# Moving loads, stores, reciprocals, rotations and late products between the steps of an attention and FFN layer

## The chip, the cores and the metric

The kernel runs on 1 core of one Trainium2 chip. The metric is the device time of one execution, in microseconds (us). The engines are called as the profile calls them: PE (TensorE, matmuls), PEld (its weight loads), DVE (VectorE), ACT (ScalarE), POOL (GpSimd), SP (SyncE, which here issues every DMA). "SPq" is SP's queue.

## What is computed

One pre-norm transformer layer over 8 sequences of 512 tokens with 512 features: attention with low-rank projections of queries, keys and values (16 heads, 128 features without and 64 with rotary position), then a gated FFN with weights rounded to 8 bits. Cut to what matters:

```python
def attn(h, wq_a, q_norm_w, wq_b, wkv_a, kv_norm_w, wkv_b, wo):   # h: 8 x 512 x 512
    q = rmsnorm(h @ wq_a.T, q_norm_w)                             # 384
    q_nope, q_pe = split((q @ wq_b.T).reshape(b, s, 16, 192), 128)
    kv_c, k_pe = split(h @ wkv_a.T, 128)
    k_pe = rope(k_pe)                                             # one for all heads
    k_nope, v = split((rmsnorm(kv_c, kv_norm_w) @ wkv_b.T).reshape(b, s, 16, 256), 128)
    q_pe = rope(q_pe)
    scores = einsum("bqhd,bkhd->bhqk", cat(q_nope, q_pe), cat(k_nope, k_pe)) / sqrt(192)
    out = einsum("bhqk,bkhd->bqhd", softmax(scores), v)
    return out.reshape(b, s, 2048) @ wo.T

def ffn(x, ...):                                                  # wq: weights rounded to e4m3
    return ((silu((x @ gate_wq) * gate_s) * ((x @ up_wq) * up_s)) @ down_wq) * down_s

x = x + attn(layernorm(x), ...)
x = x + ffn(layernorm(x), ...)
```

## The kernel before

The kernel does the attention of all 8 batches first (`attention`) and then the FFN of all 8 (`ffn`). The weights of queries and keys, and of values and output, are multiplied together in batch 0 (`fold_q`, `fold_o`), so that scores and products run on the latents themselves. The layer's input and the attention's result pass through DRAM.

**Steps.** Attention is one loop over 512 steps, `steps = (batch, head, tile of 128 queries)`: 64 steps a batch, 4 a head. Step numbers below count from the start of a batch. In each step the function `scores` puts three matmuls of 512 columns on PE (L529 and, for the rotary part in two halves, twice L531), a maximum over keys on DVE (`nmax`, L533) and the exponential with its sum on ACT (L536). The `rest` of a step, the reciprocal of the sum (L540), the scaling (L541) and a transpose in 32 x 32 blocks (L163), is recorded at the beginning of the next step. After every second tile, so at the start of even steps, `send` writes the block of transposed probabilities to DRAM (`way<-block`, L173) and reads it back in its final place in four DMAs (`prT<-way`, L175).

**All else is hung onto steps.** `put(i, f)` adds a piece of work to step i, to be recorded after that step's scores, in the order of the `put` calls; `at(b, h, t)` gives a step's number. The loop runs inside `manual_schedule`: the order in which instructions are recorded is the order of every engine's queue, and of SP's. The pieces that the change touches:

- `attend(b, h)` multiplies a head's probabilities with the values (`av`, L552), 5 steps after its last tile, and needs both halves of `prT`.
- `project` (qn, L517) and `project_pe` (qpe, L489) make the next queries. `project_pe` runs 6 steps before an even head, for two heads, and calls `rope` at once: a shuffle and two products on DVE (L394 to L396), a sum on POOL (L397). `hi` (ACT, L500) and `lo` (DVE, L505) then split the result in two parts, one step later each.
- `output(b, g)` makes, per group of 4 heads, seven products (Strassen's scheme: u, z, u, v, u, v, u; 4 matmuls of 256 columns each, L597), each followed on DVE by a sum into the batch's x (L601). A product u needs the sum of the u before it, as both use one PSUM buffer. They stand 7, 8, 12 and 15 steps after the group's last tile. For group 0 the first ones are in steps 22 and 23. `store` writes x to DRAM after the last group, at 13 and 16.
- `latents(b)` makes the next batch's latents during this batch: `moments` (L141), `deviation` (Sqrt on ACT, reciprocal on DVE, step 18), centring, transposing and projecting tile by tile (heads 7, 8, 11, 12), `norms` (Sqrt on ACT and reciprocal on DVE, L448 to L451, step 52), `scale` (L454, L457, steps 53 and 54), `transpose_l` (`lat_pt` on PE, L464, steps 54 and 55), `rotary` for the keys (step 56).
- `round_piece` rounds one half of an FFN weight tile in batches 1 to 6, every 4 steps: load, `first` (DVE and POOL), the rest (L81 and L82, DVE), and a store (L381). Its input and output tiles alternate in two buffers, so L82 of a piece must wait for the store of the piece before.
- `load_wst` fetches a group's output weights (1.8 MB in four DMAs, two buffers); `load_x` fetches a batch's x in four tiles, once as `x` (residual) and once as `tok` (for the latents of the next batch, or, in the last batch, for the first FFN).
- `load_ffn` fetches rounded weights: `wg` in the last batch, the first half of `wu` (1.5 MB) in its last step.

PSUM has eight buffers: six in a ring (`ps_r`) for everything in attention but the products, one for u, one for v and z. In `ffn`, each of 12 slices has a gate and an up product (8 matmuls each, L817) in PSUM pools of their own, then the down products (L843).

Of the kernel before, what the change touches and what calls it, by code (L numbers as in the profile page):

```python
# [43 lines left out]
P = 128  # L44
# [42 lines left out]
class Layer:  # L87
    def __init__(self, ctx, tc, ins, out):
        self.tc, self.nc, self.ins, self.out = tc, tc.nc, ins, out
        nc = self.nc  # L90
        self.wp = ctx.enter_context(tc.tile_pool(name="w", bufs=1))
        self.xp = ctx.enter_context(tc.tile_pool(name="x", bufs=1))
# [38 lines left out]
    def ln_stats(self, x, small):  # L131
# [16 lines left out]
        return moments, deviation, mv, rstd  # L148

# [30 lines left out]
    def ffn_stats(self, x, small):  # L180

        moments, deviation, mv, rstd = self.ln_stats(x, small)
        for t in range(NT):
            moments(t)
        deviation()

# [13 lines left out]
    def ffn_normed(self, x, small, psum, work):  # L200
# [3 lines left out]
        yh, yl = self.ffn_parts()  # L204
        moments, deviation, mv, rstd = self.ln_stats(x, small)
        got = {}
# [12 lines left out]

        return moments, deviation, apply, transpose, (yh, yl)  # L220

    def ffn_normed_blocks(self, x, y, small, work):
# [27 lines left out]
        return stats, apply, send, split, (yh, yl)  # L250

    def attention(self):
        tc, nc, ins, wp, xp = self.tc, self.nc, self.ins, self.wp, self.xp
        with ExitStack() as ctx:
            fp = ctx.enter_context(tc.tile_pool(name="a_f", bufs=2))
            hp = ctx.enter_context(tc.tile_pool(name="a_h", bufs=2))
            sp = ctx.enter_context(tc.tile_pool(name="a_s", bufs=4))

            ps_r = ctx.enter_context(tc.tile_pool(name="ps_r", bufs=6, space=PSUM))
            ps_o = ctx.enter_context(tc.tile_pool(name="ps_o", bufs=1, space=PSUM))  # L260
# [141 lines left out]
            def latents(b):  # L402
# [11 lines left out]
                got = {}  # L414
                moments, deviation, mv, rstd = self.ln_stats(x, sp)

# [51 lines left out]
                def rotary():  # L468
# [8 lines left out]
                    f.__name__: f  # L477
                    for f in (moments, deviation, center, transpose_x, project_x, norms, scale, transpose_l, rotary)
                }
                return pieces, (lat, kvt, kpe)  # L480

            def project_pe(b, pair):
# [14 lines left out]
                def hi():  # L497
                    qpe = state["pe", b, pair] = hp.tile([P, 2, S], F32R, tag="qpe", name="qpe")
                    for k in range(2):
                        nc.scalar.copy(qpe[half[k], k, :], rotated[half[k]])  # L500

                def lo():
                    qpe = state["pe", b, pair]
                    for k in range(2):
                        nc.vector.tensor_tensor(  # L505
                            qpe[half[1 - k], k, :], rotated[half[k]], qpe[half[k], k, :], ALU.subtract
                        )

                return hi, lo

# [134 lines left out]
            for t in range(1, NT):  # L645
                p0["moments"](t)
            p0["deviation"]()
            for t in range(NT):
# [3 lines left out]
                p0["project_x"](t)  # L652
            p0["norms"](), p0["scale"](0)
            for t in range(NT):
# [65 lines left out]

            def put_stats(b, moments, deviation):
                for t, i in enumerate((at(b, 3), at(b, 3, 1), at(b, 3, 3), at(b, 4, 1))):
                    put(i, moments, t)
                put(at(b, 4, 2), deviation)

            def put_latents(b):
                p, state["latents", b] = latents(b)
                put_stats(b - 1, p["moments"], p["deviation"])
                for t, h in enumerate(tile_heads):
                    put(at(b - 1, h), p["center"], t)  # L730
                    put(at(b - 1, h, 1), p["transpose_x"], t)
                    put(at(b - 1, h, 3), p["project_x"], t)
                put(at(b - 1, 13), p["norms"])
                for t in range(NT):
                    put(at(b - 1, 13, 1) + t // 2, p["scale"], t)
                    put(at(b - 1, 13, 2) + t // 2, p["transpose_l"], t)
                put(at(b - 1, 14), p["rotary"])

            def put_ffn():
                moments, deviation, apply, transpose, self.y = self.ffn_normed(self.fx[0], sp, ps_r, hp)  # L740
                put_stats(B - 1, moments, deviation)
                for t, h in enumerate(tile_heads):
# [4 lines left out]
            for b in range(1, B + 1):  # L747
                to, key, src = (toks, b, hidden(b)) if b < B else (self.fx, 0, self.x2[0])
                for k, f in enumerate(load_x(to, key, src, wp, "tok")):
                    put(at(b - 1, 2, 1) + 2 * k, f)  # L750
                put(at(b - 1, 3), *((put_latents, b) if b < B else (put_ffn,)))
            for g in range(NG):
                put(at(B - 1, G * g + 3, 1), self.load_ffn, "wg", g, wp, f"wa{g}")
            put(at(B - 1, NH - 1, 3), self.load_ffn, "wu", 0, wp, "wst", 2)

            with tc.manual_schedule():
                prT = block = rest = None
                for i in range(len(steps) + 17):
                    if rest:
# [21 lines left out]
    def ffn(self):  # L781
        tc, nc, ins, xp = self.tc, self.nc, self.ins, self.xp
        with ExitStack() as ctx:
            wp = ctx.enter_context(tc.tile_pool(name="f_w", bufs=1))
            qp = ctx.enter_context(tc.tile_pool(name="f_q", bufs=2))
            ps_g = ctx.enter_context(tc.tile_pool(name="ps_g", bufs=2, space=PSUM))
            ps_u = ctx.enter_context(tc.tile_pool(name="ps_u", bufs=2, space=PSUM))
            ps_d = ctx.enter_context(tc.tile_pool(name="ps_d", bufs=2, space=PSUM))

            gs, us, ds = self.gs, self.us, self.load_w("ds", pool=wp)  # L790
# [9 lines left out]
            for b in range(B):  # L800
# [10 lines left out]
                for i in range(NI):  # L811
                    pg = ps_g.tile([P, S], F32, tag="g", name="pg")
                    pu = ps_u.tile([P, S], F32, tag="u", name="pu")
                    for ps, name in ((pg, "wg"), (pu, "wu")):
                        for c in range(NC):
                            for k in range(2):
                                nc.tensor.matmul(  # L817
                                    ps,
                                    w[name, i][:, c * P : (c + 1) * P],
                                    y[k][:, c, :],  # L820
                                    start=c == 0 and k == 0,
                                    stop=c == NC - 1 and k == 1,
                                )
                    gate = qp.tile([P, S], F32, tag="gate", name="gate")
# [14 lines left out]
                for t in range(NT):  # L839
                    pd = ps_d.tile([P, H], F32, tag="d", name="pd")  # L840
                    for i in range(NI):
# [76 lines left out]
```

## Time and profile before

| | us |
|---|---|
| three timed runs | 2830.87, 2823.72, 2834.58 (median 2830.87) |
| the profiled execution | 2823.94, of it 2822.2 in the span of the profile |
| attention (until the last product on values) | about 2283 |
| FFN | about 540 |
| one batch of attention | about 280 |
| DVE busy in the span | 1862.8 |
| ACT busy in the span | 902.9 |

A line of the profile's groups or of its timeline has the engine, the line of the kernel, the operation, and its result and sources; "x8" is a number of instructions, and each fp32 matmul counts as two. What stands in brackets at the end is the idle time before it on its engine, and what ended that wait. Three groups show how the attention's inner work looks (busy us, mean ns of one, idle us before them and its releaser):

```profile
L531 PE MATMUL sc<-kpe,qpe 128*128 128x512 f32 x1024 | 526.4, 595 | 2.1 <-DVE qpe L505 2.1
L552 PE MATMUL av<-prT,kvt 128*128 128x512 f32 x1024 | 469.3, 601 | 27.4 <-DMA prT<-way 24.6
L163 DVE STREAM_TRANSPOSE block<-pr 128x512 f32<-128x512 f32 x512 | 364.3, 711 | 17.7
```

### The profile page before, as it was taken

To read this page: it belongs to the slowest core of one execution; us is meant where nothing else is said; L and a number is where in the kernel's file an instruction comes from. 1 tells how busy PE (TensorE), PEld (TensorE's weight loads), DVE (VectorE), ACT (ScalarE), POOL (GpSimd) and SP (SyncE) were. 2 spreads that over 40 slices of the span, in tenths; PEclk is the share of its full clock that TensorE was granted. 3 is DMA by queue.
4 is the path that set the end of the run, shared out by engine and by line. 5 is a ranking of instruction groups with operands and counts; after the bars stand their busy time and mean duration, and the time that the engine had idled before them with its cause. 6 is when DMAs were issued, how large, how long until landed. Compare 5 with 4: busy or idle time off the path is not lost.

```text
span 2822.2 us, 29110 instructions
## 1 busy us (share of the span) xinstructions
PE 2739.9 (97%) x9264; PEld 1724.0 (61%) x9264; DVE 1862.8 (66%) x3680; ACT 902.9 (32%) x1956; POOL 575.5 (20%) x629
## 2 busy tenths in 40 slices
PE   8999999999999999999999999999999979999999
PEld 4555555555555555655555555555555568888887
DVE  5766777777777777777777777777767724343332
ACT  3333333333333333333333333333332323332222
POOL 1222222112221222122212221222111112222222
PEclk9999999999999999999999999999999989999999
DMA  3655465546544654465446545554565542111110
GB/s 113 208 185 166 159 199 174 161 145 200 180 147 157 196 176 146 157 197 175 146 160 197 173 144 170 188 173 146 163 199 181 175 170 81 60 60 64 64 64 19
DMA packets 262376, 426.07 MB, mean 151 GB/s; under 512 B 29648, under 2 KB 192592, under 8 KB 260688
## 3 DMA queue, kind: packets, MB, share of 16 engines
q1 hardware_dynamic: 262224, 424.21, 46.5%
q8 instruction: 74, 1.21, 0.2%
q14 instruction: 78, 0.64, 0.1%
HBM read 248.99 MB, written 175.11 MB: 150 GB/s over the span
## 4 chain that ended last, share of the span: by engine, by line
PE 84%; DVE 8%; DMA 4%; ACT 1%; SPq 1%; issue 1%; POOL 0%; ACTq 0%; DVEq 0%; POOLq 0%
PE av L552 14%; PE sc L529 12%; PE qn_ps L517 9%; PE u_ps L597 7%; PE sc L531 7%; PE pg L817 6%; PE pd L843 6%; PE pu L817 6%; PE qpe_ps L489 5%; PE lr_ps L431 4%; PE v_ps L597 4%; DMA way<-block 2%; PE z_ps L597 2%; DVE pr L541 1%; DVE block L163 1%; DVE nmax L533 1%
## 5 line engine op out<-in xcount | busy, mean ns | idle before, releaser
L536 ACT ACTIVATE pr<-sc,nmax 128x512 f32<-128x512 f32 x512 | 352.0, 687 | 1270.2 <-DVE nmax L533 1270.1
L531 PE MATMUL sc<-kpe,qpe 128*128 128x512 f32 x1024 | 526.4, 595 | 2.1 <-DVE qpe L505 2.1
L529 PE MATMUL sc<-lat,qn 128*128 128x512 f32 x1024 | 524.2, 593 | 1.1 <-ACT qn L519 1.1
L552 PE MATMUL av<-prT,kvt 128*128 128x512 f32 x1024 | 469.3, 601 | 27.4 <-DMA prT<-way 24.6
L533 DVE TENSOR_REDUCE nmax<-sc 128x1 f32<-128x512 f32 x512 | 337.9, 660 | 74.0 <-PE sc L531 72.8
L163 DVE STREAM_TRANSPOSE block<-pr 128x512 f32<-128x512 f32 x512 | 364.3, 711 | 17.7
L541 DVE TENSOR_SCALAR pr<-pr,rden 128x512 f32<-128x512 f32 x512 | 343.1, 670 | 18.1
L517 PE MATMUL qn_ps<-lat,wa 128*128 128x512 f32 x768 | 350.3, 592 | 0.0
L531 PEld LDWEIGHTS sc<-kpe,qpe 128*128 128x128 f32 x1024 | 194.7, 190 | 248.0 <-issue 238.1
L552 PEld LDWEIGHTS av<-prT,kvt 128*128 128x128 f32 x1024 | 195.9, 192 | 231.7 <-issue 221.4
L529 PEld LDWEIGHTS sc<-lat,qn 128*128 128x128 f32 x1024 | 189.5, 190 | 141.1 <-issue 120.3
L397 POOL TENSOR_TENSOR roped<-rope_own,rope_sw 128x512 f32<-128x512 f32 x72 | 91.7, 1274 | 697.5 <-DVE rden L540 620.2
L517 PEld LDWEIGHTS qn_ps<-lat,wa 128*128 128x128 f32 x768 | 145.3, 189 | 134.5 <-issue 123.0
L831 POOL TENSOR_TENSOR fl<-fuse,fh 128x512 fp32r<-128x512 f32 x96 | 126.2, 1314 | 386.2 <-ACT fh L830 386.2
L827 DVE SCALAR_TENSOR_TENSOR fuse<-pu,us,gate 128x512 f32<-128x512 f32 x96 | 71.9, 749 | 197.8 <-PE pu L817 193.1
L489 PE MATMUL qpe_ps<-lat,wqp 128*128 128x512 f32 x384 | 175.1, 592 | 0.0
L76 POOL TENSOR_TENSOR q_r<-raw,q_m 128x256 f32<-128x256 f32 x72 | 53.3, 740 | 594.8 <-DVE q_m L74 530.7
L540 DVE RECIPROCAL rden<-den 128x1 f32<-128x1 f32 x512 | 80.3, 157 | 121.5 <-ACT pr L536 118.0
L817 PE MATMUL pg<-yh,wg 128*128 128x512 f32 x384 | 149.6, 390 | 0.0
L817 PE MATMUL pg<-yl,wg 128*128 128x512 f32 x384 | 149.4, 389 | 0.0
L817 PE MATMUL pu<-yh,wu 128*128 128x512 f32 x384 | 149.4, 389 | 0.0
L817 PE MATMUL pu<-yl,wu 128*128 128x512 f32 x384 | 149.4, 389 | 0.0
(115 smaller groups left out, 3674.1 us busy)
## 6 DMA issues: line engine op xcount, KB each, us to landing
way<-block SPq DMA_DIRECT2D x256, 512.0 KB, 2.6
prT<-way SPq DMA_DIRECT2D x1024, 128.0 KB, 2.8
wst<-wst_d SPq DMA_DIRECT2D x56, 512.0 KB, 4.5
wst<-wst_d SPq DMA_DIRECT2D x56, 384.0 KB, 3.7
x<-in_hid SPq DMA_DIRECT2D x60, 256.0 KB, 4.1
x<-x SPq DMA_DIRECT2D x16, 512.0 KB, 4.6
out<-o SPq DMA_DIRECT2D x32, 256.0 KB, 2.0
wst_d<-wst SPq DMA_DIRECT2D x8, 896.0 KB, 4.6
```

The source lines that it names most:

```text
L163: self.nc.vector.transpose(out[:, :, :, i : i + Q].rearrange("p c k i -> p k c i"), x.rearrange("p (k c j) -> p k c j", c=NQ, j=Q),)
L489: nc.tensor.matmul(ps, wqp_s[g][:, r, pj * P : (pj + 1) * P], lat[:, r, :], start=r == 0, stop=r == NR - 1)
L517: nc.tensor.matmul(ps, wa_s[g][:, j, r, :], lat[:, r, :], start=r == 0, stop=r == NR - 1)
L529: nc.tensor.matmul(sc, qn[:, q], lat[:, NR, :], start=True, stop=False)
L531: nc.tensor.matmul(sc, qpe[:, h % 2, q], kpe[:, part, :], start=False, stop=part == 1)
L533: nc.vector.tensor_reduce(nmax, sc, AX.X, ALU.max, negate=True)
L536: nc.scalar.activation(pr, sc, AF.Exp, bias=nmax, accum_out=den)
L541: nc.vector.tensor_scalar(pr, pr, rden, None, ALU.mult)
L552: nc.tensor.matmul(av, kvt[:, kt, :], prT[:, :, :, kt, :], start=kt == 0, stop=kt == NT - 1)
L597: nc.tensor.matmul(got[name][:, t, :], ops[p][left][:, t * P : (t + 1) * P], w[:, p, right, :], start=first and t == 0 and p == 0, stop=la ...
L817: nc.tensor.matmul(ps, w[name, i][:, c * P : (c + 1) * P], y[k][:, c, :], start=c == 0 and k == 0, stop=c == NC - 1 and k == 1,)
L843: nc.tensor.matmul(pd, f[:, i, t * P : (t + 1) * P], w["wd", i], start=i == 0 and f is fh, stop=i == NI - 1 and f is fl,)
```

## The change

It moves work between steps; PE, DVE, ACT and the DMAs do the same operations on the same data.

- Loads of `wst` come 8 steps later, `tok` 8 steps earlier (steps 1, 3, 5, 7), the four tiles of `x` in steps 17, 18, 20, 21 instead of 16 to 19.
- The stores of rounded weights come one step earlier, x's last store one step later.
- `deviation` and `norms` lose their reciprocals to `deviation_inverse` and `norms_inverse`, one step later. The four `scale` stay; `transpose_l` and `rotary` come one step later.
- `project_pe` returns `rotate, hi, lo`, so that each comes one step later.
- In the last batch, three of the seven products of group 2 go to steps 65 and 66, behind the last scores. The first part of `wu` is loaded in step 66, and in step 67, ahead of the last `attend` (step 68), the gate products of FFN slices 0 and 1 are computed with the new function `hidden`. `ffn` uses them when it comes to these slices.
- The six-buffer PSUM ring now belongs to the layer and also serves the FFN, in place of three pools of two.

```diff
+    def hidden(self, name, i, y):
+        ps = self.ps_r.tile([P, S], F32, tag="r", name="pg" if name == "wg" else "pu")
+        for c in range(NC):
+            for k in range(2):
+                self.nc.tensor.matmul(
+                    ps,
+                    self.ffn_w[name, i][:, c * P : (c + 1) * P],
+                    y[k][:, c, :],
+                    start=c == 0 and k == 0,
+                    stop=c == NC - 1 and k == 1,
+                )
+        return ps
...
         def deviation():
             nc.scalar.activation(sd, mv[:, :, 1], AF.Sqrt, bias=self.eps_ln)
+
+        def deviation_inverse():
             nc.vector.reciprocal(rstd, sd)
...
+                def norms_inverse():
                     nc.vector.reciprocal(rms, rms)
...
-                rotated = rope(ps, 1.0)
+                rotated = []
+
+                def rotate():
+                    rotated.append(rope(ps, 1.0))
...
                     def rotary_part():
-                        hi, lo = project_pe(b, h // 2)
-                        put(i - 5, hi)
-                        put(i - 4, lo)
+                        for k, f in enumerate(project_pe(b, h // 2)):
+                            put(i - 5 + k, f)
...
-                        for n, f in zip((7, 8, 12, 13, 15, 16), output(b, g)):
+                        when = (7, 8, 18, 13, 19, 17) if (b, g) == (B - 1, NG - 2) else (7, 8, 12, 13, 15, 17)
+                        for n, f in zip(when, output(b, g)):
                             put(i + n, f)
...
-                        put(at(b, G * g + 3, 3) - 14 + 2 * k, f)
+                        put(at(b, G * g + 3, 3) - 6 + 2 * k, f)
                 for k, f in enumerate(load_x(xs, b, hidden(b), xp, "x")):
-                    put(at(b, 4) + k, f)
+                    put(at(b, 4, 1) + k + k // 2, f)
...
-                for d, f in zip((-2, 0, 3, 5), round_piece(w, i, half)):
+                for d, f in zip((-2, 0, 3, 4), round_piece(w, i, half)):
                     put(at(b + 1, n + 2, 1) + d, f)
...
                 put(at(b, 4, 2), deviation)
+                put(at(b, 4, 3), deviation_inverse)
...
                 put(at(b - 1, 13), p["norms"])
+                put(at(b - 1, 13, 1), p["norms_inverse"])
                 for t in range(NT):
                     put(at(b - 1, 13, 1) + t // 2, p["scale"], t)
-                    put(at(b - 1, 13, 2) + t // 2, p["transpose_l"], t)
-                put(at(b - 1, 14), p["rotary"])
+                    put(at(b - 1, 13, 3) + t // 2, p["transpose_l"], t)
+                put(at(b - 1, 14, 1), p["rotary"])
...
-                    put(at(b - 1, 2, 1) + 2 * k, f)
+                    put(at(b - 1, 0, 1) + 2 * k, f)
...
-            put(at(B - 1, NH - 1, 3), self.load_ffn, "wu", 0, wp, "wst", 2)
+            put(at(B - 1, NH - 1, 3) + 3, self.load_ffn, "wu", 0, wp, "wst", 2)
+            self.gates = {}
+            put(
+                at(B - 1, NH - 1, 3) + 4,
+                lambda: self.gates.update((i, self.hidden("wg", i, self.y)) for i in range(2)),
+            )
...
-                for i in range(len(steps) + 17):
+                for i in range(len(steps) + 18):
...
+                    pg = self.gates.pop(i) if self.gates.get(i) else self.hidden("wg", i, y)
+                    pu = self.hidden("wu", i, y)
```

More of the change, by code (lines that the diff above doesn't have):

```diff
@@ L91, in __init__ @@
         self.wp = ctx.enter_context(tc.tile_pool(name="w", bufs=1))
+        self.ps_r = ctx.enter_context(tc.tile_pool(name="ps_r", bufs=6, space=PSUM))
         self.xp = ctx.enter_context(tc.tile_pool(name="x", bufs=1))
@@ L145, in deviation @@
             nc.scalar.activation(sd, mv[:, :, 1], AF.Sqrt, bias=self.eps_ln)
+        def deviation_inverse():
             nc.vector.reciprocal(rstd, sd)
-        return moments, deviation, mv, rstd
+        return moments, deviation, deviation_inverse, mv, rstd
     def ln_transposed(self, xn, psum):
@@ L180, in ffn_stats @@
     def ffn_stats(self, x, small):
-        moments, deviation, mv, rstd = self.ln_stats(x, small)
+        moments, deviation, deviation_inverse, mv, rstd = self.ln_stats(x, small)
         for t in range(NT):
             moments(t)
-        deviation()
+        deviation(), deviation_inverse()
         def apply(t, out):
@@ L204, in ffn_normed @@
         yh, yl = self.ffn_parts()
-        moments, deviation, mv, rstd = self.ln_stats(x, small)
+        *stats, mv, rstd = self.ln_stats(x, small)
         got = {}
@@ L218, in transpose @@
             nc.vector.tensor_tensor(yl[:, :, q], pt, yh[:, :, q], ALU.subtract)
-        return moments, deviation, apply, transpose, (yh, yl)
+        return stats, apply, transpose, (yh, yl)
     def ffn_normed_blocks(self, x, y, small, work):
@@ L257, in attention @@
             sp = ctx.enter_context(tc.tile_pool(name="a_s", bufs=4))
-            ps_r = ctx.enter_context(tc.tile_pool(name="ps_r", bufs=6, space=PSUM))
+            ps_r = self.ps_r
             ps_o = ctx.enter_context(tc.tile_pool(name="ps_o", bufs=1, space=PSUM))
@@ L414, in latents @@
                 got = {}
-                moments, deviation, mv, rstd = self.ln_stats(x, sp)
+                moments, deviation, deviation_inverse, mv, rstd = self.ln_stats(x, sp)
                 def center(t):
@@ L477, in latents @@
                     f.__name__: f
-                    for f in (moments, deviation, center, transpose_x, project_x, norms, scale, transpose_l, rotary)
+                    for f in (
+                        moments, deviation, deviation_inverse, center, transpose_x, project_x,
+                        norms, norms_inverse, scale, transpose_l, rotary,
+                    )
                 }
@@ L499, in hi @@
                     for k in range(2):
-                        nc.scalar.copy(qpe[half[k], k, :], rotated[half[k]])
+                        nc.scalar.copy(qpe[half[k], k, :], rotated[0][half[k]])
                 def lo():
@@ L505, in lo @@
                         nc.vector.tensor_tensor(
-                            qpe[half[1 - k], k, :], rotated[half[k]], qpe[half[k], k, :], ALU.subtract
+                            qpe[half[1 - k], k, :], rotated[0][half[k]], qpe[half[k], k, :], ALU.subtract
                         )
-                return hi, lo
+                return rotate, hi, lo
             def project(b, h):
@@ L646, in attention @@
                 p0["moments"](t)
-            p0["deviation"]()
+            p0["deviation"](), p0["deviation_inverse"]()
             for t in range(NT):
@@ L652, in attention @@
                 p0["project_x"](t)
-            p0["norms"](), p0["scale"](0)
+            p0["norms"](), p0["norms_inverse"](), p0["scale"](0)
             for t in range(NT):
@@ L714, in attention, with put_stats @@
                 b, n = divmod(k, 12)
-                for d, f in zip((-2, 0, 3, 5), round_piece(w, i, half)):
+                for d, f in zip((-2, 0, 3, 4), round_piece(w, i, half)):
                     put(at(b + 1, n + 2, 1) + d, f)
             tile_heads = (7, 8, 11, 12)
-            def put_stats(b, moments, deviation):
+            def put_stats(b, moments, deviation, deviation_inverse):
                 for t, i in enumerate((at(b, 3), at(b, 3, 1), at(b, 3, 3), at(b, 4, 1))):
@@ L724, in put_stats @@
                 put(at(b, 4, 2), deviation)
+                put(at(b, 4, 3), deviation_inverse)
             def put_latents(b):
                 p, state["latents", b] = latents(b)
-                put_stats(b - 1, p["moments"], p["deviation"])
+                put_stats(b - 1, p["moments"], p["deviation"], p["deviation_inverse"])
                 for t, h in enumerate(tile_heads):
@@ L733, in put_latents @@
                 put(at(b - 1, 13), p["norms"])
+                put(at(b - 1, 13, 1), p["norms_inverse"])
                 for t in range(NT):
                     put(at(b - 1, 13, 1) + t // 2, p["scale"], t)
-                    put(at(b - 1, 13, 2) + t // 2, p["transpose_l"], t)
-                put(at(b - 1, 14), p["rotary"])
+                    put(at(b - 1, 13, 3) + t // 2, p["transpose_l"], t)
+                put(at(b - 1, 14, 1), p["rotary"])
             def put_ffn():
-                moments, deviation, apply, transpose, self.y = self.ffn_normed(self.fx[0], sp, ps_r, hp)
-                put_stats(B - 1, moments, deviation)
+                stats, apply, transpose, self.y = self.ffn_normed(self.fx[0], sp, ps_r, hp)
+                put_stats(B - 1, *stats)
                 for t, h in enumerate(tile_heads):
@@ L753, in attention @@
                 put(at(B - 1, G * g + 3, 1), self.load_ffn, "wg", g, wp, f"wa{g}")
-            put(at(B - 1, NH - 1, 3), self.load_ffn, "wu", 0, wp, "wst", 2)
+            put(at(B - 1, NH - 1, 3) + 3, self.load_ffn, "wu", 0, wp, "wst", 2)
[3 more added lines that the diff above has]
+                lambda: self.gates.update((i, self.hidden("wg", i, self.y)) for i in range(2)),
+            )
             with tc.manual_schedule():
                 prT = block = rest = None
-                for i in range(len(steps) + 17):
+                for i in range(len(steps) + 18):
                     if rest:
@@ L785, in ffn @@
             qp = ctx.enter_context(tc.tile_pool(name="f_q", bufs=2))
-            ps_g = ctx.enter_context(tc.tile_pool(name="ps_g", bufs=2, space=PSUM))
-            ps_u = ctx.enter_context(tc.tile_pool(name="ps_u", bufs=2, space=PSUM))
-            ps_d = ctx.enter_context(tc.tile_pool(name="ps_d", bufs=2, space=PSUM))
             gs, us, ds = self.gs, self.us, self.load_w("ds", pool=wp)
@@ L811, in ffn @@
                 for i in range(NI):
[L812 to L823, printed above, removed]
+                    pg = self.gates.pop(i) if self.gates.get(i) else self.hidden("wg", i, y)
+                    pu = self.hidden("wu", i, y)
                     gate = qp.tile([P, S], F32, tag="gate", name="gate")
@@ L839, in ffn @@
                 for t in range(NT):
-                    pd = ps_d.tile([P, H], F32, tag="d", name="pd")
+                    pd = self.ps_r.tile([P, H], F32, tag="r", name="pd")
                     for i in range(NI):
```

## The prediction

> **What bounds the kernel now.** I read the page first, then the table of waits of PE, then windows around the waits, then the timeline at one wait of each kind. The page:
>
> ```profile
> span 2822.2 us, 29110 instructions
> PE 2739.9 (97%) x9264; PEld 1724.0 (61%) x9264; DVE 1862.8 (66%) x3680; ACT 902.9 (32%) x1956; POOL 575.5 (20%) x629
> PE   8999999999999999999999999999999979999999
> ```
>
> PE is the bound: 2739.9 of 2822.2 us. A change that leaves PE's work as it is can win the 82 us in which PE is idle, and what PE loses by running slowly. So the question is which waits those are.
>
> ```profile
> PE av L552 <- DMA prT<-way: 24.6, 8, 14.2
> PE u_ps L597 <- DVE x L601: 20.9, 6, 4.9
> PE lat_pt L464 <- DVE x L454: 14.3, 7, 2.2
> PE ln_pt L155 <- DVE xc L419: 5.1, 1, 5.1
> PE av L552 <- DMA x<-in_hid: 2.3, 1, 2.3
> ```
>
> Columns: total us, times, longest. Seven waits on L454 are one per batch whose latents are made inside the loop; six on L601 are one in each of batches 1 to 6; of the DMA's 24.6, 14.2 is one wait at the end of attention. The ln_pt wait lies in the prologue, which the change leaves in its order.
>
> ```profile
> 420.00:430.00 10.00, 5.06 (x15) 4.08 (x15) 7.73 (x15) 2.81 (x7) 1.51 (x2) 0.66 0.54 177
> 845.00:849.00 4.00, 3.94 (x12) 3.08 (x13) 3.32 (x9) 1.62 (x4) 0.35 (x1) 0.58 0.32 131
> 2265.00:2283.00 18.00, 6.41 (x8) 2.69 (x9) 0.00 (x0) 0.00 (x0) 0.00 (x0) 0.53 0.42 137
> ```
>
> Windows: length, busy us of PE, PEld, DVE, ACT, POOL, granted PE clock, DMA share, GB/s. After a wait the clock falls to half. The loss is (1 - clock) x length x PE's busy share: 1.7, 1.65 and 3.0 us in these three. I asked for nine such windows in the batches (the first two and those at 968, 1125, 1262, 1528, 1545, 1821 and 2088 us); they add up to 16.5 us.
>
> How the wait of a product comes about, in the timeline of batch 1:
>
> ```profile
> 405.32 0.42 SPq L173 DMA_DIRECT2D way<-block  x1
> 411.58 1.74 SPq L175 DMA_DIRECT2D prT<-way  x4
> 413.84 0.43 SPq L381 DMA_DIRECT2D wgd<-done  x1
> 417.10 0.42 DVE L82 SCALAR_TENSOR_TENSOR done<-q_m,q_r 128x256 fp32r<-128x256 f32 x1 [4.12 <-DMA wgd<-done]
> 424.22 0.67 DVE L601 TENSOR_TENSOR x<-x,u_ps 128x512 f32<-128x512 f32 x1
> 425.03 3.75 PE L597 MATMUL u_ps<-wst,sums 128*128 128x256 f32 x8 [4.94 <-DVE x L601]
> ```
>
> The scratch write way<-block takes 6.3 us until prT<-way can be issued, because x and wst loads share the DMA. SP works in order, so the store wgd<-done behind it goes late; its buffer is what L82 wants; DVE stands for 4.12 us with the sums of the products behind; PE waits 4.94 us and then runs slowly.
>
> The tail:
>
> ```profile
> 2257.47 0.34 SPq L173 DMA_DIRECT2D way<-block  x1
> 2261.29 1.91 SPq L175 DMA_DIRECT2D prT<-way  x4
> 2263.30 0.37 SPq L127 DMA_DIRECT2D wu<-wud  x1
> 2263.77 0.38 SPq L173 DMA_DIRECT2D way<-block  x1
> 2272.19 1.75 SPq L175 DMA_DIRECT2D prT<-way  x4
> 2276.59 6.67 PE L552 MATMUL av<-prT,kvt 128*128 128x512 f32 x8 [14.16 <-DMA prT<-way]
> ```
>
> The last way<-block stands behind a 1.5 MB load of wu and takes 8.4 us instead of 2.6 to 3.8.
>
> **What the Trainium skill says.** "TensorE: Matmul & The Clock Gate", section What's actually happening: PE's clock is halved after an idle window of some 3.4 us that runs freely. The trace agrees on the halving, and shows it after shorter waits too: the 845 us window follows a wait of about 2 us. The same page, Architectural detail (the array is 16x 32x32): ACT and DVE take their queues strictly in order; that is the L82 case above. "DMA: Bandwidth & Descriptors", Queues, rings and completion order: descriptors on each of the 16 engines are consumed in ring order, so a load issued first delays a later write; 6.3 and 8.4 us against 2.6 agree. "ScalarE: Activation LUTs", What ACT_TABLE_LOAD costs: about 1283 ns; the trace has 1.28 us before each Sqrt and again before the next Exp.
>
> **The change, part by part.** PE's instructions are the same in number; none is added. A step of the loop is about 4.4 us (280 us a batch, 64 steps).
>
> Norms and scaling. Before, the rms reciprocal stands in DVE's queue in step 52, right behind the Sqrt on ACT: DVE idles 23.7 us in 8 times for it (waits of DVE), the scaling is late, and lat_pt waits. After, the reciprocal is in step 53, and the transposes of the latents in 55 and 56 instead of 54 and 55. They get 4.4 us more, twice the longest wait (2.2). All 14.3 us go. Late next would be qpe's matmuls in step 58, which read the copied latents: a full step behind, so nothing. Moving the rotary part of the keys to step 57 leaves 7 steps to its first use.
>
> Rotation of q. Before, DVE idles for qpe_ps in the same step (85.4 us in 51 times, up to 1.9). After, it runs a step later, three steps before use instead of four. In the new step, 3 of 8, PE spends only 1.32 us, and the rotation costs DVE 2.1 us (0.73, 0.68, 0.69). Worked through with the durations of batch 2, steps 66 to 71 (rotation after the maximum of step 67 at 622.3, halves subtracted in step 69): the first sum of the products would end near 635.4, against 636.3 before, as the idle 1.9 is gone. So I take nothing, with bounds of -0.9 and +2.1 us for each of 32 groups of heads. The slack before PE's next use of u_ps there is 0.8 to 2.2 us. The PSUM buffer of qpe_ps is held one step longer: six buffers, about 1.6 taken a step, so PE's next use is still three steps off; nothing.
>
> Stores of the rounded weights one step earlier. In front of the write of that step's block rather than behind it, so L82 finds its buffer three steps later instead of two. Its waits on the three stores (18.0, 14.5 and 8.2 us of DVE in the answer on that line, all in batches 1 to 6) go. What SP has to wait for in a store, L82 of the step before, stands ahead of the block's transposes on DVE anyway, so no block is sent later.
>
> Loads. tok moves from steps 9 to 15 to steps 1 to 7, which also ends the 13.1 us in which DVE waits for it in L141; wst moves eight steps later (first group: 9 to 15), and x lies at 17, 18, 20, 21 without wst beside it. Bytes are equal. Each wst load still comes 7 steps ahead of its product. A cost: x's first piece now stands straight behind the x store on SP, without a send between, and must see that store land (4.6 us): SP is held perhaps 2 to 3 us, once a batch. The block held up is used four steps or more later; nothing, or at worst 2 us for 7 batches.
>
> From both of these and the rotation: of the 20.9 us on L601 I take 17, leaving 4 for step 54, where both pairs of scalings now meet a sum. Of the DMA waits without the tail (24.6 - 14.2 + 2.3 = 12.7), 9, since 3 us in batch 0 belong to the crowded start. Of the 16.5 us of slow clock, 15: no wait, no halving.
>
> The tail. Three products of PE work (u and v, 3.46 us, and u, 1.73) leave steps 59 and 62 and stand after the last scores, with 16 gate matmuls at 0.227 us (3.63). From the last lines: scores of step 61 begin at 2249.4 for 2252.9; three scores, 3.9, end at 2253.3. The product on head 14 then needs its prT: DVE's transpose of step 59 ends at about 2249.5, 2.7 to land, 4.4 from issue to use: 2256.6, a wait of 3.3. Its matmuls 3.44, products 5.19, gates 3.63: 2268.9. DVE's chain takes 2.9 us a step (nmax at 2257.36 and 2260.27): last transpose near 2261.3; without wu in front, 2.7 + 4.4 more: 2268.5. So the last product on values ends near 2272.3 instead of 2283.1, and 3.6 us of gates are done: 14.4. If the 3.3 us wait halves the clock, 1.7 less. I take 14. wu now waits for the last product on its buffer, is issued near 2266 and lands by 2275; first needed after seven products, at 2284: hidden.
>
> Sum: 14.3 + 17 + 9 + 15 + 14 = 69 us. Against the profiled execution's 2823.94: 2755. The median of the three runs is 6.9 us above that execution, the lowest equals it; I add half: 2758.
>
> **The rivals.** Waits move rather than vanish (x behind its store, wst in steps 9 to 15 where av of step 16 looks on): half of the L601 and DMA gain and of its clock is lost, (17 + 9 + 12) / 2 = 19: 2777. For it: the DMA share is 0.6 in these stretches. Against: in groups 2 and 3 of each batch wst runs in the same place, alone, without a wait.
>
> DVE stays late at step 22 although the store is early, by the rotation in the short step: 17 + 12 us come back: 2787. Against it: the working above.
>
> Slower: the rotation in the short step makes the first sum late in every group. At the upper bound, 2.1 less the smallest slack 0.8 is 1.3 us, plus 1.7 of halved clock: 3.0 x 32 = 96: 2854. It decides from 2.7 us a group (69 + 7 of the median + 14 for the half per cent, less what was added: about 87 / 32). DVE's idle 1.9 us in front of today's rotation speaks against it.
>
> That the late products or gates do not fill the gap: if PE meets the wait all the same, the tail gives 5 rather than 14; inside the range.
>
> **How the numbers follow.** Forecast 2758: 0.70. Waits move: 0.17. Late at step 22: 0.07. Slower: 0.03, and 0.03 for the same mechanism at half to full break-even, no change. A measurement of this kernel can tell some 0.5%, 14 us. Faster 0.94, same 0.03, slower 0.03. Low end: everything gone (14.3 + 20.9 + 12.7 + 16.5 + 17.2 = 81.6) with the median's offset 2746, and 2 for noise: 2744. High end: the second rival, 2788.
>
> **What would show it.** Right: no lat_pt wait on L454's successor; no wait of u_ps in batches 1 to 6; L82's successor without waits on stores; granted clock near 0.995; the last av about 11 us earlier, with gates before it. Wrong: waits of u_ps in all groups (rotation), sc waiting for qpe, or av waiting on DMA near steps 16 to 24 of each batch.

## The result, and the profile after

The changed kernel took 2800.7 us (median of 4 runs, 2799.5 to 2801.9) against 2828.2 us before (median of 4): a ratio of 0.9901, 95% interval 0.9879 to 0.9923. It is faster, by 28 us (1%, clear of the noise) and not by the forecast 70.

The page of the kernel after:

```profile
span 2800.0 us, 29251 instructions
PE 2728.4 (97%) x9264; PEld 1717.8 (61%) x9264; DVE 1887.1 (67%) x3680; ACT 899.0 (32%) x1956; POOL 604.1 (22%) x629
```

PE is still idle for 72 us. DVE and POOL do the same work in 24 and 29 us more. Where PE waits (total us, times, longest):

```profile
PE av L578 <- DMA prT<-way: 19.7, 8, 5.1
PE u_ps L623 <- DVE x L627: 16.2, 6, 2.9
PE u_ps L623 <- issue: 8.0, 6, 1.3
PE av L578 <- ACT pr L562: 3.7, 1, 3.7
```

Lines have moved, those in this table by 26: L578 is `attend`, L623 the products, L627 their sums. The waits of lat_pt inside the loop are gone. The six waits of u_ps at step 23 are still there, 16.2 instead of 20.9 us, but not for the store: DVE now never idles in front of L82 (which has kept its number), but it idles for the raw loads of the rounding (11.8 us for raw<-in_wu, 5.7 for raw<-in_wd). There is a new wait of 1.33 us at step 55 in six batches, put down to "issue". And the product on values at step 20 waits longer: 10.4 us in batches 1 to 6 together, where it was 6.5, and 5.1 us in batch 7, where it was 2.3. SP in steps 15 to 18 of batch 2:

```profile
666.54 0.43 SPq L379 DMA_DIRECT2D wst<-wst_d  x1
667.07 0.38 SPq L391 DMA_DIRECT2D raw<-in_wu  x1
667.54 0.38 SPq L177 DMA_DIRECT2D way<-block  x1
673.03 1.74 SPq L179 DMA_DIRECT2D prT<-way  x4
674.82 0.43 SPq L631 DMA_DIRECT2D x<-x  x1
678.50 0.35 SPq L288 DMA_DIRECT2D x<-in_hid  x1
678.95 0.38 SPq L398 DMA_DIRECT2D wgd<-done  x1
679.38 0.42 SPq L177 DMA_DIRECT2D way<-block  x1
```

The block of steps 14 and 15, sent at 667.54 behind a wst and a raw load, takes 5.5 us until prT<-way can be issued; the wait at step 20 is for this prT. After it, SP stands for 3.2 us between the store x<-x and the first load of x, which needs that store landed (22.5 us in 7 times in SP's waits); all that follows is late with it. PE waits in the same batch at step 20 and step 23:

```profile
677.53 3.67 PE L578 MATMUL av<-prT,kvt 128*128 128x512 f32 x8 [1.77 <-DMA prT<-way]
694.04 1.97 PE L623 MATMUL u_ps<-wst,sums 128*128 128x256 f32 x8 [2.85 <-DVE x L627]
```

### The profile page after: what moved, and what is told of

Its sections match the earlier page's. It is cut to its first block, busy times and chain, and to the rows that moved or that the text cites. A ratio compares the mean times of both kernels' runs of the same rounds, so it can differ in the third digit from the quotient of the medians.

```text
span 2800.0 us, 29251 instructions
## 1 busy us (share of the span) xinstructions
PE 2728.4 (97%) x9264; PEld 1717.8 (61%) x9264; DVE 1887.1 (67%) x3680; ACT 899.0 (32%) x1956; POOL 604.1 (22%) x629
## 4 chain that ended last, share of the span: by engine, by line
PE 85%; DVE 7%; DMA 4%; SPq 1%; issue 1%; ACT 1%; POOL 0%; ACTq 0%; POOLq 0%; DVEq 0%
PE av L578 13%; PE sc L555 13%; PE qn_ps L543 10%; PE u_ps L623 7%; PE sc L557 7%; PE pu L261 6%; PE pd L864 6%; PE pg L261 6%; PE qpe_ps L511 5%; PE lr_ps L448 4%; PE v_ps L623 4%; DMA way<-block 2%; PE z_ps L623 2%; DVE pr L567 2%; DVE block L167 1%; DMA raw<-in_wu 1%
## 5 line engine op out<-in xcount | busy, mean ns | idle before, releaser
L578 PE MATMUL av<-prT,kvt 128*128 128x512 f32 x1024 | 471.1, 603 | 28.9 <-DMA prT<-way 19.7
L567 DVE TENSOR_SCALAR pr<-pr,rden 128x512 f32<-128x512 f32 x512 | 334.3, 653 | 18.0
L578 PEld LDWEIGHTS av<-prT,kvt 128*128 128x128 f32 x1024 | 196.2, 193 | 234.6 <-issue 215.0
L76 POOL TENSOR_TENSOR q_r<-raw,q_m 128x256 f32<-128x256 f32 x72 | 67.5, 938 | 512.3 <-DVE q_m L74 512.3
L623 PE MATMUL u_ps<-wst,sums 128*128 128x256 f32 x512 | 126.3, 391 | 24.2 <-DVE x L627 16.2
```

The lines of the kernel that those rows point to most:

```text
L567: nc.vector.tensor_scalar(pr, pr, rden, None, ALU.mult)
L578: nc.tensor.matmul(av, kvt[:, kt, :], prT[:, :, :, kt, :], start=kt == 0, stop=kt == NT - 1)
L623: nc.tensor.matmul(got[name][:, t, :], ops[p][left][:, t * P : (t + 1) * P], w[:, p, right, :], start=first and t == 0 and p == 0, stop=la ...
```

## The experiments

Each run is compared with the kernel before on the same chip, so the differences are more exact than the times. The runs d2, d3 and d4 also have the shared PSUM ring. It adds nothing: from the end of the last product on values to the end of the span, the kernel before, d1 (without the ring), d2 and d4 (with it) all take 538.9 us.

| run | median us | less than before | ratio (95% interval) |
|---|---|---|---|
| the change | 2800.7 | 27.5 | 0.9901 (0.9879 to 0.9923) |
| d1_loads: loads and stores alone | 2800.7 | 28.1 | 0.9902 (0.9880 to 0.9923) |
| d2_norms: norms and scaling alone | 2799.9 | 28.9 | 0.9905 (0.9885 to 0.9924) |
| d3_tail: late products and gates alone | 2816.5 | 12.3 | 0.9955 (0.9938 to 0.9973) |
| d4_rotate: rotation alone | 2850.6 | -21.6 | 1.0079 (1.0062 to 1.0095) |
| e5_rotate_back: all but the rotation | 2764.3 | 64.7 | 0.9771 (0.9757 to 0.9786) |
| e7_halves_late: rotation back, halves late | 2777.0 | 52.8 | 0.9814 (0.9798 to 0.9831) |
| e8_halves_early: rotation late, halves back | 2789.3 | 40.5 | 0.9853 (0.9838 to 0.9868) |
| e1_store_back | 2797.8 | 30.6 | 0.9892 (0.9871 to 0.9913) |
| e2_raw_early | 2789.9 | 38.5 | 0.9857 (0.9834 to 0.9881) |
| e3_wst_between | 2772.3 | 56.1 | 0.9804 (0.9787 to 0.9821) |
| e4_scale_split | 2795.7 | 32.7 | 0.9887 (0.9869 to 0.9906) |
| c1_all: e1 to e4 and u, v in step 63 | 2768.4 | 60.4 | 0.9786 (0.9771 to 0.9802) |
| c3_rot_wst_uv: e5, e3 and u, v in step 63 | 2757.6 | 71.3 | 0.9747 (0.9732 to 0.9761) |
| c4_all_rot: c1 and e5 | 2754.7 | 74.2 | 0.9738 (0.9723 to 0.9752) |

**First: single repairs of the changed kernel.** I began with the DMAs, as the trace after shows SP late, against the rival that DVE has too much to do.

e1_store_back, x's last store before a send again:

```diff
-(7, 8, 12, 13, 15, 17)
+(7, 8, 12, 13, 15, 16)
```

> x's last store goes back from step 16 to step 15, so that a send stands between it and x's first load again; all else as in the changed kernel (2800.7 us). Theory A (SP's queue: the load waits on SP for the store to land, 22.5 us in 7 times, and all DMAs behind it come late, the raw loads of the rounding too): the wait of SP on the store goes, DVE waits less for raw (17.5 us in all before), PE's waits of u_ps for sums fall from 16.2 us to under 8, and the time falls by 8 to 15 us, to about 2789. Theory B (DVE itself has too much to do in steps 19 to 22, and its wait for raw is incidental): no change within 3 us.

```profile
PE av L578 <- DMA prT<-way: 27.8, 9, 4.8
PE u_ps L623 <- issue: 8.0, 6, 1.3
```

In the waits of PE the u_ps waits for DVE are gone, raw waits are down from 17.5 to 6.4 us, as theory A has it. But the store now stands in front of step 16's block, and av waits on prT take 27.8 us instead of 19.7. The gain is 3 us, not 8 to 15, and no more than the noise, as the two intervals overlap: a wait changed its place.

e2_raw_early:

```diff
-zip((-2, 0, 3, 4), round_piece(w, i, half))
+zip((-4, 0, 3, 4), round_piece(w, i, half))
```

> The raw loads of the rounding are issued four steps ahead of their use instead of two; all else as in the changed kernel. Theory A: DVE's waits for raw (17.5 us) go, u_ps waits at step 23 fall from 16.2 us to about 5, with the slow clock after them 12 to 16 us less: about 2787. Theory B: DVE no longer waits for raw but is late all the same; PE's waits of u_ps stay above 12 us, the time within 3 us of 2800.7.

```profile
PE av L578 <- DMA prT<-way: 27.0, 10, 6.8
PE u_ps L623 <- DVE x L627: 8.3, 6, 1.4
```

The waits for raw are gone and those of u_ps halved; 11 us, just short of theory A. Again av waits more.

e3_wst_between:

```diff
-put(at(b, G * g + 3, 3) - 6 + 2 * k, f)
+put(at(b, G * g + 3, 3) - 10 + 2 * k, f)
```

> The wst loads come 4 steps earlier than in the changed kernel, in steps 5, 7, 9, 11 of each group's 16 instead of 9, 11, 13, 15; all else as there. Theory A (loads that stand just ahead of a block's write on SP make the blocks of steps 14 to 16 and the last ones late): the waits of av on DMA (19.7 us, of them 5.1 and 2.7 us in the last batch and 3.7 us in the tail) fall below 9 us, the time by 10 to 15 us, to about 2788. Theory C (the DMA bandwidth is what is short, wherever the loads stand): the waits move to other steps, time within 4 us of 2800.7.

```profile
PE u_ps L623 <- DVE x L627: 23.1, 13, 2.4
PE av L578 <- DMA prT<-way: 9.8, 5, 5.1
```

28 us less than the change, twice what I expected. The av waits halved and much of the slow clock went (mean granted clock 0.997, where the change has 0.994); the waits of u_ps stay, in 13 places. The same block of batch 2 on SP, now with a raw load alone ahead of it:

```profile
665.36 0.38 SPq L391 DMA_DIRECT2D raw<-in_wu  x1
666.67 0.34 SPq L177 DMA_DIRECT2D way<-block  x1
669.34 1.74 SPq L179 DMA_DIRECT2D prT<-way  x4
```

2.7 us instead of 5.5, and the waits at step 20 are gone from batches 1 to 6, although DVE finishes the block as late as in the change. The bytes are the same, so where a load stands on SP counts, and bandwidth as such (theory C) doesn't explain the waits.

e4_scale_split:

```diff
-put(at(b - 1, 13, 1) + t // 2, p["scale"], t)
+put(at(b - 1, 13, 1) + t // 2 * 2, p["scale"], t)
```

> The second pair of scalings goes from step 54 to step 55, behind the sums of the first products; all else as in the changed kernel. If the six waits of 1.33 us (8.0 us in all) of u_ps that the profile puts down to issue are waits for DVE's sum, held up by the scalings of step 54: they go, and 7 to 8 us with them: about 2793. Rival (the transposes of step 56 or the next sums then wait): within 2 us of 2800.7.

The six waits put down to issue fall from 8.0 to 1.7 us, the time by 5, between the two theories and with intervals that overlap. In the profile, "issue" was the wait for a sum behind the second pair of scalings.

**Second: the parts of the change one by one**, on the kernel before, and all repairs together.

> The kernel before, with the moved loads and stores alone (tok in steps 1 to 7, wst in 9 to 15, x in 17 to 21, stores of the rounding one step earlier, x's last store one later). As forecast blind, this part was to take away 17 us of u_ps waits and 9 us of DMA waits and most of 16 us of slow clock: about 2792 against 2828. Theory A (the loads only change which block's write or raw load is late on SP): DMA waits of av as large as before or larger, u_ps waits of batches 1 to 6 still there, the tail later than before, as wst and wg now stand ahead of the last blocks: time between 2820 and 2838.

> The kernel before, with reciprocals, transposes of the latents and rotary part of the keys a step later alone (and one PSUM ring for attention and FFN). Blind forecast for this part: the 14.3 us of lat_pt waits and 3 us of slow clock go, 2811. Rival: half of it comes back as waits of u_ps at step 55, where the sums of the first products stand behind the late scalings (8 us in the changed kernel): about 2819.

> The kernel before, with the late products, the two gates ahead of the last product on values, the later load of wu and the shared PSUM ring alone. wst stands in its old steps, so no wst load is ahead of the last blocks. Blind forecast for this part: 14 us, 2814. Theory A: the same 12 to 15 us here, where in the whole change the last blocks are behind wst and wg loads and the part brings only about 9. Rival (DVE's chain of the last six steps is the bound of the tail, not the DMA): 8 to 9 us, 2820.

> The changed kernel with five repairs: wst loads in steps 5 to 11, x's last store back in step 15, raw loads four steps ahead, the second pair of scalings in step 55, and the late u and v products of the last batch in step 63 instead of 65, between the last scores and the product on head 14. Theory A: the repairs add up, as each frees another place of SP's or DVE's queue: u_ps waits under 5 us, av waits under 12, the tail 5 us shorter than in the changed kernel: 2752 to 2760. Theory C (bandwidth): 2770, no better than the wst repair alone.

The three parts bring 28.1, 28.9 and 12.3 us alone: 69.3 together, what the prediction's sum had for the whole. Theory A, as I put it for d1, fell as to the batches: with the loads moved and nothing else, av waits for prT in two places only, both in the last batch, one of them the tail.

```profile
PE av L552 <- DMA prT<-way: 20.9, 2, 19.2
PE lat_pt L464 <- DVE x L454: 14.3, 7, 2.1
PE u_ps L597 <- DVE x L601: 11.2, 6, 2.2
```

These are PE's waits in d1. In the batches the loads did what they were to do (20.9 to 11.2 us on sums, 10.4 to 1.7 on prT); in the tail they did harm, 19.2 us instead of 14.2, where the last group's wst now stands ahead of the last blocks on SP. c1 ended 8 us above its range, near theory C's number and 4 us below e3 alone: it left 13.5 us of waits on sums in 14 places. So repairs of the loads and scalings don't bring back what the three parts bring alone. One part was left.

**Third: the rotation.**

```diff
-                            put(i - 5 + k, f)
+                            put(i - 6 + k, f) if k else f()
```

> The changed kernel with the rotation of q (and its two halves) back in the steps where they were before; all else as in the changed kernel (2800.7 us). The three other parts, each alone on the kernel before, brought 28, 29 and 12 us, 69 together, the whole change 28. Theory R (the rotation one step later is what costs: it makes DVE some 2 us later in steps 11 to 17 of each batch, blocks and sums behind it late): 2758 to 2768, and av waits on DMA in batches 1 to 6 nearly gone. Rival O (the three parts win the same waits twice, and the rotation is neutral): 2796 to 2803.

> The kernel before with the rotation one step later alone (and one PSUM ring for attention and FFN). Blind forecast for this part: nothing, at most 2 us per batch. Theory R: slower than before by 8 to 25 us, 2837 to 2853, with waits of av on DMA around step 20 larger than before. Rival O: within 4 us of before, 2828.

> The changed kernel with the rotation back in its old step, wst in steps 5 to 11, and the late u and v products in step 63. Theory R with A: better than all so far, 2742 to 2752: the tail without wst ahead of the last blocks is 8 to 10 us shorter than with the rotation repair alone. Rival: wst beside tok in steps 5 and 7 makes blocks of the first steps late: 2760.

> As the kernel with rotation, wst and u/v products repaired, and in addition raw loads four steps ahead, x's last store back in step 15 and the second pair of scalings in step 55. If u_ps waits of some 2 us at step 23 are left there and come from late raw loads: another 5 to 12 us less, 2735 to 2745. Rival (what is left is DVE's own work in steps 19 to 22): the same within 3 us.

Rival O fell clearly. All but the rotation: 2764.3 us; the rotation alone: 21.6 us slower than before. PE's waits with the rotation alone:

```profile
PE av L578 <- DMA prT<-way: 35.2, 9, 15.0
PE u_ps L623 <- DVE x L627: 26.6, 8, 6.4
PE lat_pt L483 <- DVE x L473: 12.2, 7, 1.9
```

and with everything but the rotation:

```profile
PE u_ps L623 <- DVE x L627: 10.5, 6, 2.2
PE av L578 <- DMA prT<-way: 8.1, 4, 4.1
```

Why is DVE later, if it does the same operations and no longer idles for qpe_ps? The timeline of DVE in step 11 of batch 2, after:

```profile
644.11 0.69 DVE L559 TENSOR_REDUCE nmax<-sc 128x1 f32<-128x512 f32 x1 [0.87 <-PE sc L557]
645.84 0.69 DVE L627 TENSOR_TENSOR x<-x,u_ps 128x512 f32<-128x512 f32 x1 [1.04 <-PE u_ps L623]
647.57 0.69 DVE L627 TENSOR_TENSOR x<-x,v_ps 128x512 f32<-128x512 f32 x1 [1.04 <-PE v_ps L623]
648.18 0.73 DVE L411 STREAM_SHUFFLE rope_sw<-qpe_ps 128x512 f32<-128x512 f32 x1
650.00 0.15 DVE L566 RECIPROCAL rden<-den 128x1 f32<-128x1 f32 x1
651.81 0.71 DVE L167 STREAM_TRANSPOSE block<-pr 128x512 f32<-128x512 f32 x1
```

In step 11 PE makes the products u and v of the group before, and DVE waits for each of them to add it. The rotation stands behind both sums; the reciprocal of step 11, which could run as soon as the exponential is there (it ends at 645.6 on ACT), stands behind the rotation. The same place in e5, where the rotation has run in step 10:

```profile
643.48 0.65 DVE L559 TENSOR_REDUCE nmax<-sc 128x1 f32<-128x512 f32 x1
644.05 0.67 DVE L627 TENSOR_TENSOR x<-x,u_ps 128x512 f32<-128x512 f32 x1
644.64 0.68 DVE L627 TENSOR_TENSOR x<-x,v_ps 128x512 f32<-128x512 f32 x1
645.24 0.15 DVE L566 RECIPROCAL rden<-den 128x1 f32<-128x1 f32 x1
```

Here no sum waits. DVE comes to them later, because it rotated while PE still worked on the products. Worked out from the traces: the time from the end of a step's scores on PE to the end of its transpose on DVE, mean over batches 1 to 6, in us:

| step | before | after | e5 | e7 | e8 |
|---|---|---|---|---|---|
| 3 | 5.9 | 5.0 | 5.9 | 6.0 | 4.9 |
| 11 | 6.1 | 8.4 | 6.1 | 6.2 | 8.4 |
| 13 | 5.8 | 8.0 | 5.8 | 6.0 | 8.3 |
| 15 | 4.6 | 6.8 | 4.7 | 4.9 | 7.2 |
| 17 | 5.7 | 8.3 | 6.0 | 6.0 | 8.3 |
| 27 | 6.1 | 8.4 | 6.1 | 6.2 | 8.4 |
| 23 | 10.7 | 9.5 | 7.5 | 9.8 | 7.7 |

In step 3, where there are no products, the later rotation is even better. In steps 11 and 27 it is 2.3 us worse (steps 43 and 59, the others that are 11 of 16, lose 2.3 and 2.1). What is lost in step 11 isn't made up by step 17; moments and the rounding follow on DVE there. What is lost in step 27 is: step 31 takes 6.0 us in all five kernels. The block of steps 14 and 15 is what the product at step 20 waits for.

The lateness alone is not the price, though. In e3 and c1 the blocks of steps 11 and 15 are as late as in the change (8.4 and 6.8 us), and yet PE no longer waits for prT at step 20 of batches 1 to 6. From c1 to c4, where the rotation goes back among all other repairs, 14 us are won, not 36; c4 moves the same bytes as c1, so theory C falls here too. The waits for prT at step 20 take both: a block that is some 2 us late, and a write of it that takes 5.4 us behind wst instead of 2.8 (means of batches 1 to 6, the change and e3). Either repair ends nearly all of them.

Two more runs tell the rotation's two moves apart.

```diff
e7: -put(i - 5 + k, f)   +put(i - 5 + k, f) if k else f()
e8: -put(i - 5 + k, f)   +put(i - 5 + max(k - 1, 0), f)
```

> The changed kernel with the three DVE operations of the rotation back in the step of their matmuls, while the two halves (ACT's copy and DVE's subtraction) stay one step later, as changed. Theory R1 (the three operations in the short step, ahead of the rest of two steps' scores, make DVE late): 2762 to 2772, as with the whole rotation back (2764.3), and blocks of steps 13 to 15 end 4.6 to 6 us after their scores, as before the change. Theory R2 (the subtraction, now in the same steps 13 and 21 as the rounding of weights, is slowed by POOL and slows it): 2785 to 2801.

> The changed kernel with the rotation one step later, as changed, but the two halves in the steps where they were before the change (the copy in the step of the rotation). Theory R1: still about 2795 to 2805, blocks of steps 11 to 15 as late as in the changed kernel. Theory R2: 2764 to 2780, DVE's subtractions short again (736 ns of one instead of 857).

Neither theory has it alone. With the three operations back (e7), 24 us of the 36 come back: the blocks of steps 11 to 17 are as early as before the change, and av waits on prT take 7.3 us. With the halves back (e8), 11.5 us: av still waits 25.0 us, but the waits of u_ps for sums fall to 8.5 us. The halves' subtraction, now in steps 13 and 21, takes longer there. DVE's groups, before and after:

```profile
L505 DVE TENSOR_TENSOR qpe<-roped,qpe 64x512 fp32r<-64x512 f32 x128 | 94.2, 736 | 5.3 <-ACT qpe L500 1.6
```

```profile
L531 DVE TENSOR_TENSOR qpe<-roped,qpe 64x512 fp32r<-64x512 f32 x128 | 109.7, 857 | 5.6 <-ACT qpe L526 1.6
```

But in e8 it is hardly faster (845 ns) and the gain is there all the same, so its own length is not what counts. Two readings are left. It no longer stands in step 21, just ahead of the sums of step 22 (step 23 in the table: 9.5 and 9.8 with the halves late, 7.5 and 7.7 without). Or the rounding is no longer slowed, as theory R2 has it in its second half: POOL's operation L76 takes 938 ns in the change and 942 in e7, but 734 in e8, as before (740). No run tells the two apart.

**The best version.** c4 is 74 us faster than before and 46 faster than the change; c3, with three repairs alone, is within 3 us of it, which is within the noise. Both missed what I expected, by 6 us (c3) and 10 us (c4). The rival put for c4 held: DVE's waits for raw are gone in it, and the waits for sums are as in c3 (10.3 and 10.4 us), so late raw loads aren't their cause. The page of c4:

```profile
span 2753.5 us, 29230 instructions
PE 2715.4 (99%) x9264; PEld 1714.7 (62%) x9264; DVE 1870.2 (68%) x3680; ACT 904.3 (33%) x1956; POOL 576.3 (21%) x629
```

What is left outside the prologue and batch 0: 10.3 us of waits for sums, at step 23, one of 5.1 us at the last product on values, and one of 1.4 us at the product before it.

## Why the prediction was wrong

The reading of the bound was right: the gain was to come from PE's waits and the slow clock after them. From the kernel before to e5, PE's idle time falls from 82.2 to 43.6 us and its busy time, which holds the slow clock, from 2739.9 to 2715.7. The direction was right; the size was wrong, and this is the step that failed:

**"So I take nothing, with bounds of -0.9 and +2.1 us for each of 32 groups of heads"**, for the rotation. It measured +21.6 us alone, +36.4 in the whole change, and +14 among the other repairs (c4 to c1). I had worked it through at one place, steps 66 to 71 counted from the start of batch 1, which are steps 2 to 7 of batch 2, and that working holds: the first sum there ends 0.9 us earlier in its step, as computed (4.4 us after the start of step 6, where it was 5.3). I then took "in the new step, 3 of 8, PE spends only 1.32 us" for all of them. In every second one, step 11 of 16, PE makes two products, and the queue of DVE has two waiting sums ahead of the rotation. The blocks behind it come some 2 us late, and at step 20 PE waits for them. I had the list of what stands in which step and didn't lay it over the rotation's new place. The rival "slower", which named the right engine and the right operation, got 0.03 for the same reason: I priced it at 1.3 us with 0.8 of slack, at the sum next to it, not at the blocks it makes late. Two more rivals had a piece of it: "late at step 22", by the rotation too (0.07), and "waits move", with wst ahead of a block (0.17). I weighed them one against the other; the waits for prT at step 20 needed both. The prediction's own sign of being wrong, "av waiting on DMA near steps 16 to 24 of each batch", is what came.

**Norms and scaling**: forecast 14.3 us of waits and some 3 of slow clock, measured 28.9 alone. The mechanism was right, the term too small. Heads 13 and 14 of a batch together take 3.4 us less than before in the mean of seven batches, 24 us in all. In a batch where the clock stays full it is 3.2 us (40.9 to 37.7): 2.3 ahead of the first transpose of the latents, and 0.9 within the transposes, which stood further apart; the table of waits named 2.0 a batch. The other 5 us lie in the comparison: the profiled execution of the kernel before, with 2823.9 us, is one of its shortest, some 5 below the median. The forecast also had "leaving 4 for step 54"; with the rotation it is 8.0, at step 55; in e5, without it, no wait is seen there.

**Loads and stores**: forecast 17 + 9 us and most of 15 of slow clock, measured 28.1 alone. Stores: right, L82's wait is gone. But of the 17 us on sums only 9.7 went (20.9 to 11.2): 1.7 to 2.2 us are left at step 23 of each of batches 1 to 6, and in c4 still 1.7. That term was too large; why DVE is late there stays open, and its own work in steps 19 to 22 is what the tried theories leave. That wst does no harm in its new place was right in the batches as long as the blocks aren't late (d1), but I followed wst only through groups 0 to 2: for the last group of the last batch it is issued in steps 57 to 63, with wg in 61, ahead of the last blocks. The wait in the tail grew by 5 us (14.2 to 19.2).

**The x store**: "SP is held perhaps 2 to 3 us", measured 3.2; "nothing" as its cost was wrong as long as the blocks are late (e1: PE's waits for sums at step 23 vanish, though PE waits 8 us more for prT), and small as soon as they are not (c3, which leaves the store where the change put it, is within 3 us of c4).

**The tail**: forecast 14, measured 12.3 alone. In the whole change it is less: from step 48 of the last batch to the end it takes 617.0 us, where the kernel before takes 621.3 and d3 610.4. PE waits twice:

```profile
2240.12 6.67 PE L578 MATMUL av<-prT,kvt 128*128 128x512 f32 x8 [3.74 <-ACT pr L562]
2259.34 5.37 PE L578 MATMUL av<-prT,kvt 128*128 128x512 f32 x8 [3.69 <-DMA prT<-way]
```

The first wait, at 3.3 us in the forecast, is 3.74, but for another thing: the profile puts it down to ACT's exponential (pr), not to prT. I take it that the last scores still hold the PSUM ring; that wasn't tried. The second was forecast at nothing: the block before last takes 8.3 us behind wst and wg (sent at 2238.16, prT<-way issued at 2246.48), and the last one 6.2 behind another wst.

So the sum was 69 for the whole, and three parts bring 69.3 together when each is tried alone. That is luck: the norms bring 12 us more than forecast, the loads 8 less, the tail 2 less. With all three in one kernel and no rotation it is 64.7 (2764.3 us, inside the range). That the rotation costs 15 us more in the whole than alone fits that DVE's other waits partly hide it in the kernel before (L82's idle is 31.6 us in d4 and 40.7 before, that for the rms Sqrt 17.3 and 23.7); this is a reading of the two traces and wasn't tried by itself. That the cost falls to 14 us among the other repairs shows that it depends on what the late blocks and sums meet; where the 15 us come from stays open.

## What to carry to other kernels

When a piece of work is moved by a step on an engine that runs strictly in order, write down for every kind of step what stands ahead of it there, and whether that waits for another engine; a place worked through once is good for the steps like it only. Idle time of an engine in front of an operation isn't lost if what follows it would have had to wait anyway: DVE's 1.9 us before the old rotation were free, and the move spent them at a place where they weren't. And try the parts of a change singly: here three won 69 us and one lost 22, and in the whole that one lost 36, which the result alone doesn't tell. A delay has no fixed price: here either of two repairs, the rotation's or that of wst, took the waits at step 20 away.

## What was not expected of the hardware

The Trainium skill ("TensorE: Matmul & The Clock Gate", What's actually happening) names an idle window of about 3.4 us for the halved clock. Here shorter waits were enough, and not each time: after the change, the wait of 2.85 us at step 23 of batch 2 left the clock full (1.00 in the window from 690 to 700 us), and one of 2.91 us at the same step of batch 3 halved it for a part of the window from 967 to 977 us (0.66 in its mean). In the kernel before, a wait of 2.15 us did (the 845 us window of the prediction). So, by an estimate from the two lines below, a wait of some 3 us costs between nothing and 0.34 x 7.09 = 2.4 us more, in the same place, from batch to batch.

```profile
690.00:700.00 10.00, 7.15 (x27) 4.85 (x26) 9.08 (x17) 1.56 (x4) 1.61 (x2) 1.00 0.58 182
967.00:977.00 10.00, 7.09 (x20) 5.38 (x19) 6.39 (x12) 1.56 (x4) 1.06 (x1) 0.66 0.74 226
```
